# A 256-state scan: GpSimd relieved by VectorE every 64 steps, and LayerNorm's sums taken by ScalarE while it copies and squares

## The chip, the cores and the metric

The kernel runs on one core of a Trainium2 chip. A core has five engines that work side by side, each with its own queue of instructions in program order: PE (TensorE, matrix products), DVE (VectorE), ACT (ScalarE, functions of one operand), POOL (GpSimd) and SP (SyncE, which here only issues DMAs). Semaphores tie the queues together: an instruction waits at the head of its queue until what it needs is done, and everything behind it in that queue waits too. The metric is the device time of one execution in microseconds; lower is better. Before the change it is 21432.37 us (median of 3 runs, 21429.57 to 21440.76).

## The reference, cut to what matters

Two layers on an image batch of shape (4, 128, 64, 64), all in float32. Layer 0 is convolutions, a sort of patches and a scan with 16 states. Layer 1, in which the change lies, normalises tokens, runs a scan with 256 states for each of 256 channels over 4096 tokens, and then a long causal convolution with 16 filters:

```python
t = _to_tokens(x)                                  # (4, 4096, 128)
t = t + _L1_attn_ref(_ln_t(t), W_in, W_delta, W_B, W_C, W_out, A, D)
t = t + _L1_ffn_ref(_ln_t(t), ...)                 # the long convolution

def _ln_t(v, eps=1e-5):
    m = jnp.mean(v, axis=-1, keepdims=True)
    s = jnp.var(v, axis=-1, keepdims=True)
    return (v - m) / jnp.sqrt(s + eps)

# in _L1_attn_ref
deltaA = jnp.exp(jnp.einsum('bld,dn->bldn', delta, A))
deltaB = jnp.einsum('bld,bln->bldn', delta, Bv)
def step(state, inp):
    dA_i, dB_i, x_i, C_i = inp
    state = dA_i * state + dB_i * x_i[:, None, :]
    y = jnp.einsum('bdn,bn->bd', state, C_i)
    return (state, y)
```

## The kernel before, in words

`layer0_front` and `layer0_scan` come first and are not touched. `layer1` works on 32 parts: 4 batches by 8 chunks of 512 tokens, batches 0 and 1 one after the other, then batches 2 and 3 in turn chunk by chunk. A part has 256 steps, one for each channel d. A step scans one channel for all 256 states (128 partitions by 2 halves) over 512 tokens, so one instruction handles 1024 elements on each partition. The main loop (lines 1321 to 1370) issues, for step k:

- every second step, `fetch` (SP): the DMA that spreads two rows of delta over all partitions into `dlb` (4 buffers), for step k+8;
- at every half part, `carry` (POOL): it multiplies and adds in the state left by the chunk before;
- every second step, `spread` (line 1212, POOL): the scan's inputs v for steps k+4 and k+5, u times delta, 2 x 2 x 511 elements on each partition; v has 3 buffers of two steps each. ScalarE's small copy (line 1216) then puts the carried column in;
- `lift` (line 1232, ACT): two exponentials that make the factors da of step k+1, in one of two PSUM buffers;
- `due` (ACT): copies of finished convolutions (line 1181) that have come due;
- a piece of the step before's contraction: every 8 steps give four groups of PE products (line 1252) and two copies ye by ACT (line 1258), which are spread over steps 0 to 5 of the following eight;
- `scan` (line 1235, DVE): the scan of step k itself, which needs v and da;
- at most one piece of the work "beside": the output of the last part and the preparation (`project`) of the next. This work is written as generators. A piece marked "mm" is issued at step 6 of a group of eight, one marked "post" at step 7, and one marked "free" at any step. All "mm" pieces share a single PSUM buffer, `mm`;
- matmuls of the long convolution (line 1169, PE), as many as a credit allows.

**Relief.** GpSimd need not make all of v. At steps k with k % 128 == 118, `spread` is told to make only the first of its two steps, and `relief` makes the other: ScalarE copies the row of delta into the PSUM buffer `mm` (line 1222), and VectorE multiplies it with u (line 1224). While a relief is under way ("helping"), the "mm" piece of that group waits for the next one.

**Normalisation.** `normalise` (lines 828 to 850) is called twice a part: once by `project` for the next part's tokens, once by `output` for the tokens that go to the convolution. PE transposes the tokens into PSUM, ScalarE copies them to SBUF (lines 874 and 998), VectorE takes mean and variance of 4 rows of 128 (`bn_stats`, `bn_aggr`, lines 833 and 835), ScalarE adds eps and turns the mean's sign (838, 840), GpSimd raises to the power -1/2 and multiplies (843, 844), and after five more pieces ScalarE scales and shifts (line 848). Before the first step the first preparation runs with nothing beside it, and after the last step so does the last output.

Of the kernel before, what the change touches and what calls it, by code (L numbers as in the profile page):

```python
# [8 lines left out]
F32 = mybir.dt.float32  # L9
# [762 lines left out]
def layer1(ctx: ExitStack, tc, ident, half, weights, phi, pqd, mud, x, omd, permd, x2, x3, out):  # L772
# [52 lines left out]
    def middle():  # L825
        return pm.tile([128, TS], F32, tag="mm", name="mm")

    def normalise(t):

        st = sm.tile([128, NT, 6], F32, tag="st", name="st")  # L830
        mv = sm.tile([128, NT, 2], F32, tag="mv", name="mv")
        for i in range(NT):
            nc.vector.bn_stats(st[:, i, :], t[:, i, :])
        for i in range(NT):
            nc.vector.bn_aggr(mv[:, i, :], st[:, i, :])
        yield "free"
        ve = sm.tile([128, NT], F32, tag="ve", name="ve")
        nc.scalar.activation(ve, mv[:, :, 1], AF.Identity, bias=eps)
        ms = sm.tile([128, NT], F32, tag="ms", name="ms")
        nc.scalar.activation(ms, mv[:, :, 0], AF.Copy, scale=-1.0)  # L840
        yield "free"
        rs = sm.tile([128, NT], F32, tag="rs", name="rs")
        nc.gpsimd.tensor_tensor(rs, ve, half[:, :NT], ALU.pow)
        nc.gpsimd.tensor_tensor(ms, ms, rs, ALU.mult)
        for _ in range(5):
            yield "free"
        for i in range(NT):
            nc.scalar.activation(
                t[:, i, :], t[:, i, :], AF.Identity, bias=ms[:, i : i + 1], scale=rs[:, i : i + 1]
            )  # L850
# [11 lines left out]
    def project(b, ch, into):  # L862


        u, c, gate, delta, af, vf = into
        xq = small()
        nc.sync.dma_start(xq, x2[b][:, bass.ts(ch, TS)])
        yield "mm"
        tp = middle()
        for i in range(NT):  # L870
            nc.tensor.transpose(tp[:, bass.ts(i, 128)], xq[:, bass.ts(i, 128)], ident)
        yield "post"
        tr = small()
        nc.scalar.copy(tr, tp)
        yield "free"
        tr = tr.rearrange("p (i c) -> p i c", i=NT)
        yield from normalise(tr)
        yield "mm"
        ps = middle()
        for i in range(NT):  # L880
            nc.tensor.transpose(ps[:, bass.ts(i, 128)], tr[:, i, :], ident)
        yield "post"
        xn = small()
        nc.scalar.copy(xn, ps)
        z = wide()
        for j in range(2):
            yield "mm"
            ps = middle()
            nc.tensor.matmul(ps, win[:, bass.ds(256 + 128 * j, 128)], xn, start=True, stop=True)
            yield "post"  # L890
            nc.scalar.copy(z[:, j, :], ps)
        yield "free"
        nc.scalar.activation(z, z, AF.Silu)
        nc.sync.dma_start(gate, z)
        xs = wide()
        for j in range(2):
            yield "mm"
            ps = middle()
            nc.tensor.matmul(ps, win[:, bass.ts(j, 128)], xn, start=True, stop=True)
            yield "post"  # L900
            nc.scalar.copy(xs[:, j, :], ps)
        for j in range(2):
            yield "mm"
            ps = middle()
            for k in range(2):
                nc.tensor.matmul(ps, wbd[:, k, bass.ts(j, 128)], xs[:, k, :], start=k == 0, stop=k == 1)
            yield "post"
            nc.vector.tensor_tensor(u[:, j, :], ps, xs[:, j, :], ALU.mult)
        wcs = small().rearrange("p (k n) -> p k n", k=2)
        nc.sync.dma_start(wcs, wc)  # L910
        for j in range(2):
            yield "mm"
            ps = middle()
            for k in range(2):
                nc.tensor.matmul(ps, wcs[:, k, bass.ts(j, 128)], xs[:, k, :], start=k == 0, stop=k == 1)
            yield "post"
            nc.scalar.copy(c[:, j, :], ps)
            yield "mm"
            ps = middle()
            for k in range(2):  # L920
                nc.tensor.matmul(
                    ps, wbd[:, k, bass.ds(256 + 128 * j, 128)], xs[:, k, :], start=k == 0, stop=k == 1
                )
            yield "post"
            dl = small()
            nc.scalar.copy(dl, ps)
            nc.sync.dma_start(delta[bass.ts(j, 128), :], dl)

            yield "mm"
            ps = middle()  # L930
            nc.tensor.matmul(ps[:, 0:128], dl[:, 0:1].broadcast_to((128, 128)), ident, start=True, stop=True)
            yield "post"
            for h in range(2):
                nc.scalar.activation(vf[:, h, bass.ts(j, 128)], ps[:, 0:128], AF.Copy, scale=u[:, h, 0:1])
            for h in range(2):
                nc.vector.tensor_tensor(af[:, h, bass.ts(j, 128)], ps[:, 0:128], at[:, h, bass.ts(j, 128)], ALU.mult)
        yield "free"
        nc.scalar.activation(af, af, AF.Exp)
# [30 lines left out]
    def output(b, ch, yt, gate):  # L969


        cols = bass.ts(ch, TS)
        xr = small()
        nc.sync.dma_start(xr, x2[b][:, cols])
        yk = wide()
        nc.sync.dma_start(yk, gate)
        for k in range(2):
            yield "mm"
            ps = middle()
            for i in range(NT):  # L980
                nc.tensor.transpose(ps[:, bass.ts(i, 128)], yt[:, i, bass.ts(k, 128)], ident)
            yield "post"
            nc.vector.tensor_tensor(yk[:, k, :], ps, yk[:, k, :], ALU.mult)
        yield "mm"
        ps = middle()
        for k in range(2):
            nc.tensor.matmul(ps, wo[:, k, :], yk[:, k, :], start=k == 0, stop=k == 1)
        yield "post"
        nc.vector.tensor_tensor(xr, xr, ps, ALU.add)
        yield "mm"  # L990
        pair = xr.rearrange("p (a q) -> p q a", q=2)
        tp = middle()
        for r in range(2):
            for i in range(2):
                nc.tensor.transpose(tp[:, bass.ts(2 * r + i, 128)], pair[:, r, bass.ts(i, 128)], ident)
        yield "post"
        tk = small()
        nc.scalar.copy(tk, tp)
        yield "free"
        yield from normalise(tk.rearrange("p (i c) -> p i c", i=NT))  # L1000
        yield "mm"
        if ch % 2 == 0:
            tokens[b, ch // 2] = sp.tile([128, 2, 4, 128], F32, tag="tok", name="tok", bufs=6)
        tok = tokens[b, ch // 2]
        ps = middle()
        nc.tensor.matmul(ps, flip, tk, start=True, stop=True)
        yield "post"
        nc.scalar.copy(tok[:, :, bass.ts(ch % 2, 2), :], ps.rearrange("p (r i c) -> p r i c", r=2, i=2))
        yield "mm"
        up = middle()  # L1010
        for i in range(NT):
            nc.tensor.transpose(up[:, bass.ts(i, 128)], tk[:, bass.ts(i, 128)], ident)
        mu = small()[:, 0:384].rearrange("p (i c) -> p i c", i=3)
        nc.sync.dma_start(mu, mud[:, (0, 1, 2, 2, 3, 3, 3, 3)[ch]])
        yield "post"
        ut = sm.tile([128, 2 + TS], F32, tag="t2", name="ut", bufs=3)
        nc.scalar.copy(ut[:, 2:].rearrange("p (a q) -> p q a", q=2), up.rearrange("p (q a) -> p q a", q=2))
        if ch:
            nc.scalar.copy(ut[:, 0:2], halos[b % 2])
        else:  # L1020
            nc.scalar.activation(ut[:, 0:2], ident[:, 0:2], AF.Copy, scale=0.0)
        nc.scalar.copy(halos[b % 2], ut[:, TS:])
        yield "mm"
        ps = middle()
        for i in range(3):
            nc.tensor.matmul(ps, mu[:, i, :], ut[:, bass.ds(2 - i, TS)], start=i == 0, stop=i == 2)
        yield "post"
        nc.vector.tensor_tensor(xr, xr, ps, ALU.add)
        nc.sync.dma_start(x3[b][:, cols], xr)
        if (b, ch) == (NB - 1, NCH - 2):  # L1030
            add([(b, 3, [(3, range(2))], True, False)])
        elif (b, ch) == (NB - 1, NCH - 1):
            add([(b, 3, [(3, range(2, 4))], True, True)])
        elif ch % 2:
            block(b, ch // 2)
# [285 lines left out]
    for k in range(-10, steps):  # L1321
# [7 lines left out]
        j = k + 4  # L1329
        if 0 <= j < steps and j % VD == 0:  # L1330

            mine = k % 128 == 118 and kind != "post"
            vs[j // VD] = spread(j % 256, dls[j // VD], ready[j // 256], VD - mine)
            if mine:
                helping = relief(vs[j // VD], dls[j // VD], ready[j // 256])
# [127 lines left out]
```

## Time and profile before

| What | us |
|---|---|
| median of the runs | 21432.37 |
| the profiled execution | 21431.38 |
| its span, first to last instruction | 21429.6 |
| from the first scan (L1235) to the last | 2801.4 to 21249.6 |
| L1235's scans, busy | 18006.6 |
| L1212's products on POOL, busy | 18244.4 |

A line of the profile names a group of instructions by its line in the kernel, its engine and operation, what it writes and reads, and the shape on partitions by elements. Busy time is the time in which at least one of the group ran; "mean" is the average length of one, and because an engine starts an instruction while the last one finishes, it is longer than the distance from one start to the next. Idle time is that of the engine just before these instructions, with what ended it. The chain of waits is followed back from the last instruction: at each step to what released it, or to the one before it on its engine.

### The profile page before, as it was taken

The numbers are of one execution on the slowest core, as the hardware profiler recorded it, in microseconds if no ns is written. First come the engines' busy times: TensorE is split into PE (matmuls) and PEld (weight loads), VectorE is DVE, ScalarE is ACT, GpSimd is POOL, SyncE is SP. The second block draws the span as 40 slices with busy tenths as digits, with TensorE's granted clock in tenths as the row PEclk, the third lists the DMA queues.
The fourth block names the chain that finished last, engine by engine and source line by source line (L and its number), as shares of the span: only waits on it lengthen the run. The fifth ranks groups of instructions, "written<-read, shape, count | busy, mean of one in ns | idle before, by whom it ended". The sixth has DMA issues, their size and how long they took to land.

```text
span 21429.6 us, 294489 instructions
## 1 busy us (share of the span) xinstructions
PE 17672.7 (82%) x99308; PEld 7756.7 (36%) x99308; DVE 20566.6 (96%) x11871; ACT 16044.5 (75%) x29620; POOL 20134.2 (94%) x5685
## 2 busy tenths in 40 slices
PE   7788854565858888886868999599999999999997
PEld 4344421222323333342323344243434434334434
DVE  7788889999999999999999999999999999999996
ACT  3777767777777777777777777787887787788875
POOL 2677789999999999999999999999999999999996
PEclk8999966776979999998979999799999999999999
DMA  1455544555756777766657777577777777777776
GB/s 69 126 139 141 140 151 153 175 179 165 218 171 221 221 224 220 221 212 191 209 181 220 230 237 236 171 236 232 237 232 229 232 234 232 233 233 230 231 231 186
DMA packets 2498780, 4302.24 MB, mean 201 GB/s; under 512 B 803272, under 2 KB 1321712, under 8 KB 2494192
## 3 DMA queue, kind: packets, MB, share of 16 engines
q1 hardware_dynamic: 2497264, 4283.40, 65.4%
q8 instruction: 784, 12.85, 0.2%
q14 instruction: 732, 6.00, 0.1%
HBM read 3658.98 MB, written 623.38 MB: 200 GB/s over the span
## 4 chain that ended last, share of the span: by engine, by line
DVE 57%; PE 14%; POOL 9%; ACT 9%; issue 8%; DMA 3%; SPq 0%; DVEq 0%; POOLq 0%; ACTq 0%
DVE s L1235 50%; POOL v L1212 8%; PE conv L1169 6%; ACT da L1232 5%; DVE states L562 3%; PE yp L1252 3%; DVE p L566 2%; PE fin L1111 1%; ACT f L554 1%; PE y L578 1%; DMA strip<-in_phi 1%; DMA dlb<-delta 1%; PE mm L471 1%; PE conv L104 0%; DVE v L1224 0%
## 5 line engine op out<-in xcount | busy, mean ns | idle before, releaser
L1212 POOL TENSOR_TENSOR v<-u,dlb 128x2044 f32<-128x2044 f32 (+1 forms) x4096 | 18244.4, 4517 | 91.7 <-DMA dlb<-delta 66.0
L1235 DVE TENSOR_TENSOR_SCAN s<-da,v 128x1024 f32<-128x1024 f32 x8192 | 18006.6, 2264 | 188.3 <-ACT da L1232 130.3
L1232 ACT ACTIVATE da<-dlb,at 128x511 f32<-128x511 f32 x16384 | 11302.9, 690 | 1990.3 <-DVE s L1235 1488.8
L1169 PE MATMUL conv<-strip,tok 128*128 128x512 f32 (+3 forms) x20480 | 8653.3, 550 | 59.0 <-DMA strip<-in_phi 58.5
L1252 PE MATMUL yp<-s,c 128*32 128x256 f32 x65536 | 4957.0, 432 | 2616.2 <-DVE s L1235 1136.7
L1169 PEld LDWEIGHTS conv<-strip,tok 128*128 128x128 f32 x20480 | 3667.2, 192 | 4156.2 <-issue 3715.8
L1252 PEld LDWEIGHTS yp<-s,c 128*32 128x32 f32 x65536 | 1964.4, 120 | 6395.3 <-issue 2085.0
L1216 ACT COPY v<-vf 128x4 f32<-128x4 f32 x4096 | 814.2, 199 | 2112.6 <-DVE s L1235 2093.6
L1111 PE MATMUL fin<-conved,pq 128*128 128x512 f32 (+1 forms) x3968 | 1793.6, 545 | 11.1 <-ACT sum L1132 5.9
L540 POOL TENSOR_TENSOR v<-dx,bcb 128x1024 f32<-128x1024 f32 x512 | 1207.2, 2358 | 436.9 <-DVE states L562 430.5
L562 DVE TENSOR_TENSOR_SCAN states<-f,v 128x1024 f32<-128x1024 f32 x512 | 1175.8, 2297 | 172.6 <-ACT f L554 123.7
L554 ACT ACTIVATE f<-dt,an 128x255 f32<-128x255 f32 x2048 | 973.5, 476 | 418.0 <-DVE states L562 367.2
L1258 ACT COPY ye<-yp 128x512 f32<-128x512 f32 x2048 | 1186.1, 579 | 23.3 <-PE yp L1252 22.6
L1181 ACT COPY conved<-conv 128x512 f32<-128x512 f32 (+1 forms) x1728 | 986.9, 571 | 236.6 <-PE conv L1169 234.0
L578 PE MATMUL y<-p,ident 128*128 128x512 f32 x2048 | 1006.7, 620 | 148.2 <-DVE p L566 143.2
L1111 PEld LDWEIGHTS fin<-conved,pq 128*128 128x128 f32 x3968 | 664.2, 192 | 384.6 <-issue 284.2
L566 DVE TENSOR_TENSOR p<-states,bcb 128x1024 f32<-128x1024 f32 x512 | 626.9, 1224 | 41.1 <-DVE states L562 3.1
L578 PEld LDWEIGHTS y<-p,ident 128*128 128x128 f32 x2048 | 369.4, 195 | 680.9 <-issue 356.3
L471 PE MATMUL mm<-ow,yg 128*32 128x128 f32 x2048 | 283.1, 298 | 106.9 <-ACT om L475 105.4
L471 PEld LDWEIGHTS mm<-ow,yg 128*32 128x32 f32 x2048 | 236.6, 139 | 213.6 <-ACT om L475 128.5
L405 PE MATMUL mm<-xin,taps 128*128 128x512 f32 x512 | 236.6, 605 | 28.3 <-DVE f L384 14.4
L447 POOL TENSOR_TENSOR e<-e,e 128x1024 f32<-128x1024 f32 x32 | 75.1, 2346 | 191.0 <-ACT e L445 191.0
(242 smaller groups left out, 5948.1 us busy)
## 6 DMA issues: line engine op xcount, KB each, us to landing
dlb<-delta SPq DMA_DIRECT2D x4096, 512.0 KB, 4.2
strip<-in_phi SPq DMA_DIRECT2D x1536, 448.0 KB, 4.8
yd<-ye SPq DMA_DIRECT2D x2048, 256.0 KB, 4.1
strip<-in_phi SPq DMA_DIRECT2D x1088, 256.0 KB, 4.4
bcb<-bcd SPq DMA_DIRECT2D x1024, 256.0 KB, 4.1
pq<-pqd SPq DMA_DIRECT2D x1472, 64.0 KB, 3.8
yt<-yd SPq DMA_DIRECT2D x4096, 4.0 KB, 3.4
pq<-pqd SPq DMA_DIRECT2D x256, 128.0 KB, 3.9
```

Of the source, the lines that this page charges most:

```text
L540: nc.gpsimd.tensor_tensor(v, ready[n][2][:, :, bass.ts(i, SUB)].unsqueeze(1).broadcast_to((128, 2, 2, SUB)), bc[:, 0].unsqueeze(2).broadca ...
L554: nc.scalar.activation(factors[j % 2][:, a, k, 1:], ready[n][1][:, k, SUB * i + 1 : SUB * i + SUB], AF.Exp, scale=an[:, k, 2 * g + a : 2 * ...
L562: nc.vector.tensor_tensor_scan(states.rearrange(flat), factors[j % 2].rearrange(flat), v.rearrange(flat), 0.0, ALU.mult, ALU.add)
L566: nc.vector.tensor_tensor(p, states, bc[:, 1].unsqueeze(2).broadcast_to((128, 2, 2, SUB)), ALU.mult)
L578: nc.tensor.matmul(t.rearrange("p k t -> p (k t)"), ident, p[:, a].rearrange("p k t -> p (k t)"), start=g == 0 and a == 0, stop=False, ski ...
L1111: nc.tensor.matmul(fin[:, bass.ds(c0, w)], pq[:, n, :], u[:, bass.ds(c0, w)], start=begin and n == 0, stop=end and not partly, skip_group_ ...
L1169: nc.tensor.matmul(ps[:, skip:], tok[:, 1 - r if side else r, j, :], strip[:, bass.ds(c0 - lo, TS - skip)], start=which == 0 and j == js[0 ...
L1212: nc.gpsimd.tensor_tensor(v[:, 0:n, :, 1:], ready[0][:, :, 1:].unsqueeze(1).broadcast_to((128, n, 2, TS - 1)), dl[:, 0:n, 1:].unsqueeze(2) ...
L1232: nc.scalar.activation(da[:, h, 1:], dl[:, d % VD, 1:], AF.Exp, scale=at[:, h, d : d + 1])
L1235: nc.vector.tensor_tensor_scan(s[:, d % GD].rearrange("p h t -> p (h t)"), da.rearrange("p h t -> p (h t)"), v[:, d % VD].rearrange("p h t ...
L1252: nc.tensor.matmul(yp[i // 2][bass.ts(q, 32), i % 2], c[:, h, t], s[:, :, h, t], start=h == 0, stop=h == 1)
L1258: nc.scalar.copy(ye, yp[j].rearrange("p i d t -> p i t d"))
```

## The change

There are two edits. In the main loop a relief now comes every 64 steps (k % 64 == 54) and not every 128. In `normalise`, ScalarE's copy from PSUM is now made in four Identity activations, each of which also adds up its row; four Square activations, biased by the negative mean, one in each of four steps, add up the squares; the variance and eps follow from these sums in one small activation. VectorE's `bn_stats` and `bn_aggr` go, and so do the two copies of the callers, whose PSUM tile is now handed to `normalise`.

```diff
-    def normalise(t):
-
-        st = sm.tile([128, NT, 6], F32, tag="st", name="st")
-        mv = sm.tile([128, NT, 2], F32, tag="mv", name="mv")
+    def normalise(t, ps):
+
+        sums = sm.tile([128, 2, NT], F32, tag="st", name="st")
         for i in range(NT):
-            nc.vector.bn_stats(st[:, i, :], t[:, i, :])
+            nc.scalar.activation(t[:, i, :], ps[:, bass.ts(i, 128)], AF.Identity, accum_out=sums[:, 0, i : i + 1])
+        yield "free"
+        ms = sm.tile([128, NT], F32, tag="ms", name="ms")
+        nc.scalar.activation(ms, sums[:, 0, :], AF.Copy, scale=-1.0 / 128)
         for i in range(NT):
-            nc.vector.bn_aggr(mv[:, i, :], st[:, i, :])
+            yield "free"
+            sq = sm.tile([128, 128], F32, tag="sq", name="sq", bufs=1)
+            nc.scalar.activation(
+                sq, t[:, i, :], AF.Square, bias=ms[:, i : i + 1], accum_out=sums[:, 1, i : i + 1]
+            )
         yield "free"
         ve = sm.tile([128, NT], F32, tag="ve", name="ve")
-        nc.scalar.activation(ve, mv[:, :, 1], AF.Identity, bias=eps)
-        ms = sm.tile([128, NT], F32, tag="ms", name="ms")
-        nc.scalar.activation(ms, mv[:, :, 0], AF.Copy, scale=-1.0)
+        nc.scalar.activation(ve, sums[:, 1, :], AF.Identity, bias=eps, scale=1.0 / 128)
         yield "free"
...
         tr = small()
-        nc.scalar.copy(tr, tp)
-        yield "free"
         tr = tr.rearrange("p (i c) -> p i c", i=NT)
-        yield from normalise(tr)
+        yield from normalise(tr, tp)
...
         tk = small()
-        nc.scalar.copy(tk, tp)
-        yield "free"
-        yield from normalise(tk.rearrange("p (i c) -> p i c", i=NT))
+        yield from normalise(tk.rearrange("p (i c) -> p i c", i=NT), tp)
...
-            mine = k % 128 == 118 and kind != "post"
+            mine = k % 64 == 54 and kind != "post"
             vs[j // VD] = spread(j % 256, dls[j // VD], ready[j // 256], VD - mine)
```

## The prediction, made before the changed kernel ran

> **What bounds the kernel now.** Read in this order: the page's busy shares and chain, busy times by stage, groups, a stretch of the timeline. From the page:
>
> ```profile
> PE 17672.7 (82%) x99308; PEld 7756.7 (36%) x99308; DVE 20566.6 (96%) x11871; ACT 16044.5 (75%) x29620; POOL 20134.2 (94%) x5685
> ...
> DVE 57%; PE 14%; POOL 9%; ACT 9%; issue 8%; DMA 3%; SPq 0%; DVEq 0%; POOLq 0%; ACTq 0%
> DVE s L1235 50%; POOL v L1212 8%; PE conv L1169 6%; ACT da L1232 5%; DVE states L562 3%; PE yp L1252 3%; DVE p L566 2%; PE fin L1111 1%; ACT f L554 1%; PE y L578 1%; DMA strip<-in_phi 1%; DMA dlb<-delta 1%; PE mm L471 1%; PE conv L104 0%; DVE v L1224 0%
> ```
>
> DVE (VectorE) and POOL (GpSimd) look full, and the chain passes mostly through DVE's scan. The stages of the 256-state scan say more (microseconds of each engine, instructions in brackets):
>
> ```profile
> core 0: us, PE busy (x) PEld busy (x) DVE busy (x) ACT busy (x) POOL busy (x), PEclk, DMA share, GB/s
> 3000.00:12000.00 9000.00, 6642.12 (x42178) 2806.89 (x42182) 8927.65 (x4443) 6767.80 (x12456) 8978.62 (x2119) 0.85 0.64 198
> 14500.00:17000.00 2500.00, 2392.35 (x13415) 1031.04 (x13412) 2466.66 (x1235) 1995.19 (x3715) 2492.99 (x591) 0.99 0.75 233
> 19000.00:21200.00 2200.00, 2095.90 (x11923) 918.30 (x11923) 2165.56 (x1073) 1776.49 (x3279) 2184.30 (x515) 1.00 0.76 230
> ```
>
> POOL is busy 99.6 to 99.8% in every stage, DVE 98.4 to 99.2%, ACT (ScalarE) 75 to 81%, PE 74% and then 95 to 96%. The groups (busy us, mean ns | idle before, what ended it) of DVE, POOL and ACT:
>
> ```profile
> L1235 DVE TENSOR_TENSOR_SCAN s<-da,v 128x1024 f32<-128x1024 f32 x8192 | 18006.6, 2264 | 188.3 <-ACT da L1232 130.3 <-POOL v L1212 42.2
> ...
> L1224 DVE TENSOR_TENSOR v<-u,mm 128x1022 f32<-128x1022 f32 x64 | 76.2, 1190 | 0.0
> ...
> L833 DVE BATCH_NORM_STATS2 st<-t 128x6 f32<-128x128 f32 x256 | 54.0, 271 | 20.8 <-ACT t L874 19.4 <-ACT t L998 1.5
> ...
> L835 DVE BATCH_NORM_AGGREGATE mv<-st 128x2 f32<-128x6 f32 x256 | 23.0, 150 | 0.0
> ```
>
> ```profile
> L1212 POOL TENSOR_TENSOR v<-u,dlb 128x2044 f32<-128x2044 f32 (+1 forms) x4096 | 18244.4, 4517 | 91.7 <-DMA dlb<-delta 66.0 <-DVE s L1235 24.8
> ...
> L843 POOL TENSOR_TENSOR rs<-ve,half 128x4 f32<-128x4 f32 x64 | 66.4, 1037 | 73.1 <-ACT ms L840 38.5 <-ACT ve L838 34.6
> ...
> L1205 POOL TENSOR_TENSOR af<-af,last 128x256 f32<-128x256 f32 x56 | 42.8, 763 | 0.0
> L1206 POOL TENSOR_TENSOR vf<-vf,af 128x256 f32<-128x256 f32 x56 | 40.6, 725 | 4.4
> ```
>
> ```profile
> L1232 ACT ACTIVATE da<-dlb,at 128x511 f32<-128x511 f32 x16384 | 11302.9, 690 | 1990.3 <-DVE s L1235 1488.8 <-DMA yt<-yd 57.0 <-DMA strip<-in_phi 31.3
> ...
> L848 ACT ACTIVATE t<-t,ms,rs 128x128 f32<-128x128 f32 x256 | 104.7, 480 | 2.7 <-POOL ms L844 2.7
> ...
> L1222 ACT COPY mm<-dlb 128x512 f32<-128x512 f32 x64 | 36.9, 576 | 0.0
> ...
> L193 ACT ACTIVATION_READ_ACCUMULATOR f<-sum,b 128x1 f32 x32 | 5.8, 182 | 0.0
> ```
>
> Durations overlap their neighbours, so I take prices from start to start:
>
> ```profile
> 9998.36 39.34 DVE L1235 TENSOR_TENSOR_SCAN s<-da,v 128x1024 f32<-128x1024 f32 x18
> 10037.62 0.66 DVE L908 TENSOR_TENSOR u<-mm,t 128x512 f32<-128x512 f32 x1
> 10038.20 17.54 DVE L1235 TENSOR_TENSOR_SCAN s<-da,v 128x1024 f32<-128x1024 f32 x8
> ...
> 9998.86 62.86 POOL L1212 TENSOR_TENSOR v<-u,dlb 128x2044 f32<-128x2044 f32 x14
> ```
>
> 18 scans end to end take 39.26 us before the next operation starts (2.181 us each), 14 products v take 62.86 us (4.490 for two steps, 2.245 a step). So GpSimd is slower per step than the scan. DVE's extras fill the difference, or it waits for v.
>
> Sums for one part (256 steps; 32 parts, first scan at 2801.4 us, last at 21249.6 us: 18450 us, 576.6 a part):
> - POOL: 126 products x 4.49 + 2 halves x 2.31 (median) = 570.4; the powers and products of two normalisations 2 x (1.04 + 0.20) = 2.5; carries 2 x (0.76 + 0.73) = 3.0. Sum 575.9 of 576.6.
> - DVE: 256 x 2.181 = 558.4; the extras (L1224 2.4, L833 and L835 2.4, six evacuations together) 9.6 as start-to-start times. Sum 568.0. The other 8.6 are waits. Scan by scan, comparing each start with the later of its v and its da: 106 us in all for v, in 763 mostly tiny waits, 151 us for da in 182, and some 1 us a part of jitter. (The group row's 42.2 and 130.3 leave out the 0.08 us of overlap that a waiting scan loses.)
>
> By halves of the scan, in us a part: parts 0 to 15 take 575.8, with 4.3 for v and 2.8 for da; parts 16 to 31 take 577.2, with 2.4 for v and 6.7 for da, where the convolution's copies crowd ACT and PE is nearly full. In both halves POOL never rests while DVE waits for v: **POOL is the bound, and DVE is 2 to 4 us a part behind it.**
>
> **What the skill says.** GPSIMD Engine Reference, "3.1 Elementwise": a two-input fp32 tensor_tensor of 2048 elements takes 4497 ns; the trace agrees (4.49 us for 2044). Perfetto Trace Analysis, "GPSIMD Engine Instruction", wants such spans timed from start to start, as done here. SBUF — State Buffer, "SBUF: two separate sides": VectorE and GpSimd lock each other out only when VectorE uses a 2-port mode or two SBUF inputs. The added VectorE product reads u from SBUF and the copied row from PSUM, so it should not slow POOL; the trace agrees: beside L1224 a half product keeps its 2.32 us (median). ScalarE: Activation LUTs, "What ACT_TABLE_LOAD costs", is the price list used below: 186 ns + 0.833 ns an element, 93 ns more for each per-partition pointer operand, back-to-back overlap 93 ns. Trace: L848 (128 elements, two pointers) 480 ns against 479 by that rule.
>
> **The change, part by part.**
> (1) Relief every 64 steps: 64 more steps whose second half DVE makes. POOL loses 2 x (4.49 - 2.31) = 4.36 us a part, 139 us in all, from an engine without slack. DVE gains 2 x 1.11 (L1224 start to next start; mean 1.19) = 2.2 us a part. ACT gets 2 copies of 0.58 (L1222), at step 6 of a group of eight, where little else lies; each takes one of the slots in which PE's side products are issued.
> (2) bn_stats and bn_aggr leave DVE: 512 instructions. One normalisation takes 4 x 0.193 + 4 x 0.08 = 1.1 us from start to start, two a part: -2.2 us. This pays for (1) on DVE almost exactly, so DVE's own load is unchanged.
> (3) ACT's copy (0.58) becomes 4 Identity with sums, then 4 Square with sums. Identity reads PSUM, no pointer: 186 + 107 = 293 ns by the page (estimate), 0.20 start to start. Reading the accumulator adds 0.089: in the first layer the read starts 0.617 after L193's start, and the next operation 0.089 after the read. So 4 x 0.29 = 1.16. Square has one pointer: 0.29 + 0.09 = 0.38, 4 times, one a step. Bounds for an Identity: 0.25 (L934, from PSUM) to 0.385 (L848) before the read, so 0.29 to 0.47.
> When does ACT make DVE late? A lift (two L1232) takes 1.41 of a 2.18 us step, so 0.77 is left, and the two da buffers let a step run over by another 0.65 before the scan waits. On before: 4 L848 at 0.385 and a 0.11 copy leave the lift 0.82 late and cost a 0.17 stall, as the records show. The sums' step: 1.16 + 0.11 - 0.77 - 0.05 = 0.45, below 0.65: no stall, unless a convolution copy (0.5) falls in it, about one step in 8 in the first half and one in 3.3 in the second. The squares' steps hold at most a square, a ye copy and a small copy: 0.99, over by 0.2, paid back in the next step. I take 0.2 us a part of new stall in the first half, 0.5 in the second. At 0.47 an accumulating operation the sums' step stalls by 0.5, and it is 1.3 a part.
> (4) Moves. The normalisation's last step moves from step 7 to step 3 of the next group, before the same slot at step 6, so PE's next product is not later for it; the two more reliefs move what follows by one slot (8 steps), then two. In the changed kernel's own order the last piece of preparation is issued at step 215 instead of 199; the next part's rows are fetched from step 248. The DMAs are as many as before (4096 dlb, 64 delta and so on); the convolution's matmuls after the last scan also (128).  GpSimd's power waits for ve, issued one step before, as now. No table load is added (211 in both).
> (5) Where nothing covers: the preparation ahead of the first scan and the output after the last. There copy, bn and ve of 0.58 + 1.1 + 0.3 become 1.16 + 0.1 + 1.52 + 0.2, +1 us each, with hand-overs +4 in all at most; I take +3.
>
> **What is late next.** POOL falls to 571.5 (mean parts had up to 3.5 us of waits for a row's DMA: 66 us in all). DVE without waits for v, with new stalls: first half 575.8 - 4.3 + 0.2 = 571.7; second half 577.2 - 2.4 + 0.5 = 575.3. Both engines are level in the first half, and they alternate: carries fall at steps 118 and 246, the Silu's table loads (2.4 us stall) once a part, a relief every 64 steps moves 3.3 us of lead, and v's ring holds about 4.4. So I leave 1.2 us a part of waits for v in the first half, and 0.6 in the second, where POOL has room. Gain: 16 x (575.8 - 572.9) + 16 x (577.2 - 575.9) = 46 + 21 = 67, less 3: **64 us**. The profiled execution took 21431.4 (its span 21429.6), the median of the runs is 21432.4, 1 us apart, so the forecast is 21368.
>
> **The rivals.**
> - *Full gain:* all of POOL's 139 us is saved, if ACT's stalls shrink as the order shifts. Against: the second half's stalls for da (6.7 a part) are not POOL's. The 106 us and a few more: 21432 - 115 = 21317.
> - *DVE or ACT is the bound anyway:* waits for v vanish, but come back as waits for da, since a step no longer stretched by v leaves ACT less room; PE at 95% holds ye and the copies back. For it: 6.7 us a part. Then only half of the first half's gain stays: 21432 - 20 = 21412.
> - *Slower:* an accumulating activation cannot overlap with its read. The sums' step then has 4 x (0.39 + 0.18 + a drain of about 0.2), some 3 us on ACT's in-order queue, ahead of the lift for the next scan: stall 1.6, and each square 0.77, which fills its step's room and adds about 1 a normalisation in the first half and 2 in the second. Twice a part: 5 and 7 us against 3.1 and 1.8 gained: +30 and +83, 21545 at the full price. It decides from 106 / 32 = 3.3 us of new stall a part. Against it: L193's 0.089. A milder one ends near 21490.
> - *It does not do what it says:* excluded; the order shows 128 reliefs for 64, and no bn instruction in this scan.
>
> **Numbers.** About 0.2% (43 us) is what a measurement here can tell from no change. Forecast 0.60, of which a sixth lies within 43 us; full gain 0.10; bound anyway 0.15; slower 0.15, most of it beyond 43 us. Faster 0.60, same 0.25, slower 0.15. The likeliest one's own range is 21325 to 21410; the range with 8 in 10 takes in most of the full gain and of the bound case: 21310 to 21430.
>
> **What would show it.** Right: L1212 with 128 halves and about 139 us less busy time; L1235's wait for POOL v well under 42 us; POOL's busy share down to about 99%, with waits for DVE's scan; L1235's wait for ACT da 130 to 150; the reads at about 0.09 from start to start. Wrong: waits for da near 250, an Identity with sums that lasts over 0.5 us, or POOL still at 99.7% with a v slower than 4.49.

## The result, and the profile after

| What | before | after |
|---|---|---|
| median of 20 runs of each, us | 21436.17 | 21405.07 |
| the profiled execution's span, us | 21429.6 | 21403.1 |
| a part, parts 0 to 15, us | 575.79 | 573.88 |
| a part, parts 16 to 31, us | 577.23 | 577.20 |

The ratio is 0.9986, with a 95% interval of 0.998 to 0.9992: 31 us faster. The forecast was 64 us faster, so the direction was right and the time lies in the range, but half of the gain did not come. By parts the whole gain is in the first half (16 x 1.91 = 31 us, where 46 were forecast), and the second half gave nothing (21 were forecast). (The two profiled executions are 26.5 us apart: 31 in the parts, less some 4 that the two ends cost.)

First the page of the kernel after: the busy shares, then the chain by engine and by line.

```profile
PE 17645.8 (82%) x99308; PEld 7753.1 (36%) x99308; DVE 20524.2 (96%) x11423; ACT 16192.4 (76%) x30644; POOL 19986.7 (93%) x5685
...
DVE 60%; PE 14%; ACT 10%; issue 8%; POOL 4%; DMA 3%; SPq 0%; DVEq 0%; POOLq 0%; ACTq 0%
DVE s L1235 53%; PE conv L1169 6%; ACT da L1232 5%; DVE states L562 3%; POOL v L1212 3%; PE yp L1252 3%; DVE p L566 2%; PE fin L1111 1%; ACT f L554 1%; DVE v L1224 1%; DMA strip<-in_phi 1%; PE y L578 1%; ACT ye L1258 1%; PE mm L471 1%; DMA dlb<-delta 0%
```

POOL does 147 us less, and the chain passes through its products for 3% of the span in place of 8%. DVE takes the chain over. POOL is no longer the bound, as the stages show as well (busy time of each engine in each stretch, instructions in brackets):

```profile
core 0: us, PE busy (x) PEld busy (x) DVE busy (x) ACT busy (x) POOL busy (x), PEclk, DMA share, GB/s
3000.00:12000.00 9000.00, 6624.72 (x42295) 2809.56 (x42288) 8926.64 (x4248) 6864.31 (x12995) 8938.77 (x2127) 0.85 0.64 199
14500.00:17000.00 2500.00, 2386.97 (x13442) 1028.64 (x13444) 2468.96 (x1173) 2015.07 (x3856) 2477.68 (x592) 1.00 0.76 233
19000.00:21200.00 2200.00, 2096.40 (x11930) 917.51 (x11933) 2162.98 (x1025) 1793.93 (x3392) 2166.70 (x515) 0.99 0.76 230
```

POOL's share is 99.3, 99.1 and 98.5%. So it has slack now, and yet the scan still waits for it. The groups of DVE (busy us, mean ns | idle before, and what ended it), then of POOL:

```profile
L1235 DVE TENSOR_TENSOR_SCAN s<-da,v 128x1024 f32<-128x1024 f32 x8192 | 17972.6, 2292 | 194.4 <-ACT da L1232 143.3 <-POOL v L1212 42.0
...
L1224 DVE TENSOR_TENSOR v<-u,mm 128x1022 f32<-128x1022 f32 x128 | 155.2, 1212 | 0.0
```

```profile
L1212 POOL TENSOR_TENSOR v<-u,dlb 128x2044 f32<-128x2044 f32 (+1 forms) x4096 | 18097.2, 4473 | 208.9 <-DMA dlb<-delta 131.9 <-DVE s L1235 65.0 <-POOL v L1212 6.4
```

The wait for v stands at 42.0 us where it was 42.2. This row counts idle time only, and hides what changed. Scan by scan, before lost 35 us in 33 waits for v of half a microsecond or more, and 71 us in some 750 tiny ones; after loses 35 us in 24 long ones, and 22 us in some 240 tiny ones. The change took away tiny waits, which fits a POOL that could just not keep up. The long ones stayed.

On POOL, the waits for the scan (a free v buffer) rose from 24.8 to 65.0 us, which is what an engine with slack shows; but the waits for a row of delta rose too, from 66.0 to 131.9. In both sums one wait lies ahead of the first scan, that for the first row of all (timeline of POOL, before, then after; in brackets the idle time before and its releaser):

```profile
2796.85 13.41 POOL L1212 TENSOR_TENSOR v<-u,dlb 128x2044 f32<-128x2044 f32 x3 [43.81 <-DMA dlb<-delta]
2805.20 4.50 POOL L1212 TENSOR_TENSOR v<-u,dlb 128x2044 f32<-128x2044 f32 x1 [45.72 <-DMA dlb<-delta]
```

Without it the waits for rows rose from 22 to 86 us, fourfold. This is where the missing gain has to be looked for.

ScalarE's sums were as cheap as forecast. A stretch of its timeline ahead of the first scan (start us, length us; first line with its idle time before):

```profile
2754.23 0.28 ACT L832 ACTIVATE t<-mm 128x128 f32<-128x128 f32 x1 [8.34 <-PE mm L875]
2754.41 0.20 ACT L832 ACTIVATION_READ_ACCUMULATOR t<-mm 128x1 f32 x1
2754.50 0.27 ACT L832 ACTIVATE t<-mm 128x128 f32<-128x128 f32 x1
```

The read starts 0.18 us after its Identity, and the next Identity 0.09 after the read: 0.27 for this pair, with no drain in between. Over all 192 such pairs the median is 0.25.

**Where the time went.** As in the prediction, each scan's start was compared with the later of its v and its da. In us a part, worked out from the records (the scans themselves take 558.4 in every row; what is left over is jitter):

| us a part, first half / second half | period | waits for da | waits for v | DVE's other work |
|---|---|---|---|---|
| before | 575.79 / 577.23 | 3.88 / 7.39 | 4.25 / 2.36 | 8.99 / 8.87 |
| after | 573.88 / 577.20 | 3.90 / 8.11 | 2.15 / 1.46 | 9.26 / 9.14 |
| forecast for after | 572.9 / 575.9 | +0.2 / +0.5 | 1.2 / 0.6 | no change |

(Waits for da are counted more widely here than in the prediction, which had 2.8 and 6.7 for before and left the tiny waits to jitter. With only waits above 0.06 us before has 2.8 and 6.6, and after 3.3 and 7.4.) Waits for v are 0.95 and 0.86 us a part above the forecast, together 29 us of the 36 by which the parts miss their forecast (16 x 0.98 + 16 x 1.30). DVE's other work adds 0.27 a part, 9 us; ScalarE's new stalls are, in this table's count, 3 us below the forecast in the first half and 4 above it in the second.

**One late row.** The waits for v in the first half are not spread out: of 34.4 us, 33.1 lie in steps 64 to 127 of a part, and most of it in parts 2, 4, 6, 12 and 14, with 4 to 5.4 us each, while parts 1, 3, 7, 8, 10 and 15 have at most 0.6. In these parts POOL stands still once, at step 88. In part 4 (timeline of POOL, then of DVE):

```profile
5284.21 9.00 POOL L1212 TENSOR_TENSOR v<-u,dlb 128x2044 f32<-128x2044 f32 x2
5298.73 9.01 POOL L1212 TENSOR_TENSOR v<-u,dlb 128x2044 f32<-128x2044 f32 x2 [5.52 <-DMA dlb<-delta]
```

```profile
5273.73 8.82 DVE L1235 TENSOR_TENSOR_SCAN s<-da,v 128x1024 f32<-128x1024 f32 x4
5282.47 0.69 DVE L1028 TENSOR_TENSOR t<-t,mm 128x512 f32<-128x512 f32 x1
5283.07 17.55 DVE L1235 TENSOR_TENSOR_SCAN s<-da,v 128x1024 f32<-128x1024 f32 x8
5303.29 4.47 DVE L1235 TENSOR_TENSOR_SCAN s<-da,v 128x1024 f32<-128x1024 f32 x2 [2.67 <-POOL v L1212]
```

POOL waits 5.52 us for a row; DVE lives on the v buffers that were already filled until 5300.6 and then waits 2.67. Why was the row late? SP's timeline over the same time (issues of DMAs; the length is that of issuing):

```profile
5278.00 0.32 SPq L1259 DMA_DIRECT2D yd<-ye  x1
5279.87 0.32 SPq L1196 DMA_DIRECT2D dlb<-delta  x1
5283.19 0.32 SPq L1029 DMA_DIRECT2D x<-t  x1
5283.61 0.37 SPq L871 DMA_DIRECT2D t<-x  x1
5284.03 4.31 SPq L1275 DMA_DIRECT2D yt<-yd  x8
5288.39 0.43 SPq L1077 DMA_DIRECT2D pq<-pqd  x1
5288.86 0.91 SPq L1083 DMA_DIRECT2D strip<-in_phi  x2
5289.81 0.43 SPq L1077 DMA_DIRECT2D pq<-pqd  x1
5290.29 0.43 SPq L1083 DMA_DIRECT2D strip<-in_phi  x1
5290.83 1.31 SPq L1196 DMA_DIRECT2D dlb<-delta  x2
```

From 5280.2 to 5283.2 SP stands at line 1029, the write of x3: it needs VectorE's sum of line 1028, which DVE reaches only after its scans, and which ends at 5283.16. Behind that write the program queues the load of line 871, eight reads of y, filters and strips, and only then the row for steps 88 and 89. The row is issued at 5290.83, right behind these transfers, and lands late as well (chain of waits: start, length, what):

```profile
5290.83 7.75 DMA dlb<-delta
5298.57 0.02 issue
5298.60 0.04 POOLq L1212
5298.64 0.09 issue
5298.73 4.53 POOL v L1212
5303.27 0.02 issue
5303.29 4.48 DVE s L1235 x2
```

7.75 us against a median of 4.2 for these rows. Such gaps on POOL, of 4 to 7 us, are found in eight parts (2, 4, 6, 12, 14, 16, 19 and 23), 45.6 us in all. The kernel before had the same event one group earlier, at step 80, with 1.0 to 3.5 us in ten parts, 24 us in all. So the change did not make it. It moved it by 8 steps, and a POOL that runs further ahead comes to the late row sooner and waits longer for it: the rows just ahead of the late one had lain ready for 8.1 us (median) when POOL took them in before, and for 5.1 in after, and the pauses grew by 1.6 to 4.5 us (the eight parts without part 16).

**Why in these parts.** SP stands at the write for 2.5 to 4.1 us in most parts, and in eight of those (1, 3, 7, 8, 10, 11, 15 and 18) POOL pauses for at most 0.3 us. What sets the eight apart is what follows the write. Worked out from the records of after (medians, us; part 0 has no such write, and for five rows the landing is not on record):

| loads of filters and strips between the write and the row | parts | SP stands at the write | from the write to the row's issue | row in flight | POOL's pause, least to most |
|---|---|---|---|---|---|
| none | 12 | 2.3 | 4.8 | 4.4 | 0 to 0.6 |
| one or two | 11 | 3.0 | 5.7 | 6.1 | 0 to 3.2 |
| four to six | 8 | 3.5 | 7.3 | 7.4 | 4.1 to 6.3 |

The last row of this table is exactly the eight parts. In `output`, the call that gives the convolution new work stands right behind the write, in every second chunk; in parts 4, 6, 12, 14 and 19 the convolution's matmuls (line 1169) had stood still for 310 to 780 us when it came. Its first loads then go out in one burst, ahead of the row. Where it was still at work, as in parts 8 and 10, there is no burst. So three things add up: a write that waits for VectorE, the reads and loads that are issued behind it, and a longer flight.

### The profile page after: what moved, and what is told of

It reads as the page before. It is cut to its first block, busy times and chain, and to the rows that moved or that the text cites. A ratio compares the mean times of both kernels' runs of the same rounds, so it can differ in the third digit from the quotient of the medians.

```text
span 21403.1 us, 295158 instructions
## 1 busy us (share of the span) xinstructions
PE 17645.8 (82%) x99308; PEld 7753.1 (36%) x99308; DVE 20524.2 (96%) x11423; ACT 16192.4 (76%) x30644; POOL 19986.7 (93%) x5685
## 3 DMA queue, kind: packets, MB, share of 16 engines
q14 instruction: 736, 6.03, 0.1%
## 4 chain that ended last, share of the span: by engine, by line
DVE 60%; PE 14%; ACT 10%; issue 8%; POOL 4%; DMA 3%; SPq 0%; DVEq 0%; POOLq 0%; ACTq 0%
DVE s L1235 53%; PE conv L1169 6%; ACT da L1232 5%; DVE states L562 3%; POOL v L1212 3%; PE yp L1252 3%; DVE p L566 2%; PE fin L1111 1%; ACT f L554 1%; DVE v L1224 1%; DMA strip<-in_phi 1%; PE y L578 1%; ACT ye L1258 1%; PE mm L471 1%; DMA dlb<-delta 0%
## 5 line engine op out<-in xcount | busy, mean ns | idle before, releaser
L1212 POOL TENSOR_TENSOR v<-u,dlb 128x2044 f32<-128x2044 f32 (+1 forms) x4096 | 18097.2, 4473 | 208.9 <-DMA dlb<-delta 131.9
L1235 DVE TENSOR_TENSOR_SCAN s<-da,v 128x1024 f32<-128x1024 f32 x8192 | 17972.6, 2292 | 194.4 <-ACT da L1232 143.3
```

Of the source, the lines that this page charges most:

```text
L1212: nc.gpsimd.tensor_tensor(v[:, 0:n, :, 1:], ready[0][:, :, 1:].unsqueeze(1).broadcast_to((128, n, 2, TS - 1)), dl[:, 0:n, 1:].unsqueeze(2) ...
L1235: nc.vector.tensor_tensor_scan(s[:, d % GD].rearrange("p h t -> p (h t)"), da.rearrange("p h t -> p (h t)"), v[:, d % VD].rearrange("p h t ...
```

## The experiments

My theory when these began: the missing gain is the late row; the write of x3 in front of it is the cause. The rivals: the two halves of the change do not fit together (one of them alone gives all of the 31 us, or costs), DVE or ScalarE is the bound in any case, or too little was moved from POOL. Each run was timed together with the kernel before on the same chip; its medians were 21443.67 in the group of e1 to e4, 21442.15 for e5, e6 and e8, and 21442.61 for e9 and e10, each group on another chip. "Against before" below is the difference from the median of the same group.

| Kernel | median us | ratio to before (95%) | against before | v waits | da waits | DVE's other work |
|---|---|---|---|---|---|---|
| e1_relief_only | 21443.22 | 0.9999 (0.9991 to 1.0007) | -0.5 | 1.05 | 5.62 | 11.15 |
| e2_sums_only | 21433.82 | 0.9995 (0.9987 to 1.0003) | -9.9 | 4.92 | 5.76 | 6.99 |
| e3_after_late_write | 21360.67 | 0.9961 (0.9948 to 0.9975) | -83.0 | 0.46 | 6.03 | 9.21 |
| e4_before_late_write | 21424.27 | 0.9991 (0.9982 to 0.9999) | -19.4 | 2.87 | 5.85 | 8.93 |
| e5_relief_48 | 21393.88 | 0.9978 (0.997 to 0.9986) | -48.3 | 0.15 | 5.65 | 10.67 |
| e6_split_scale | 21355.44 | 0.9959 (0.9945 to 0.9972) | -86.7 | 0.44 | 5.46 | 9.21 |
| e8_tanh_gate | 21305.41 | 0.9937 (0.9925 to 0.995) | -136.7 | 0.48 | 2.60 | 10.33 |
| e9_sums_late | 21412.63 | 0.9986 (0.9979 to 0.9992) | -30.0 | 4.18 | 5.83 | 6.99 |
| e10_relief_late | 21399.79 | 0.998 (0.9972 to 0.9988) | -42.8 | 0.13 | 5.46 | 11.15 |

The last three columns are us a part over all 32 parts, worked out as above; before has 3.31, 5.64 and 8.93, after has 1.81, 6.01 and 9.20.

### The two halves of the change, each alone

e1 is the kernel before with the relief every 64 steps; e2 is the kernel after with the relief every 128:

```diff
# e1, on before
-            mine = k % 128 == 118 and kind != "post"
+            mine = k % 64 == 54 and kind != "post"
# e2, on after
-            mine = k % 64 == 54 and kind != "post"
+            mine = k % 128 == 118 and kind != "post"
```

> The relief every 64 steps alone, with the old normalisation (bn_stats on VectorE). Theory (GpSimd and VectorE are level, so each half of the change needs the other): GpSimd loses 4.4 us a part, but VectorE gains 2.2 us a part and becomes the bound; no gain, -10 to +25 us against before (21436). L1212's busy time falls by about 147 us, as with both. Rival (the relief brings the whole gain): about -31 us.

> ScalarE's sums alone, with the old relief every 128 steps. Theory (GpSimd stays the bound, VectorE's 2.0 us a part that go turn into waits for v): -10 to +10 us against before; L1235's waits for v grow from 3.3 us to about 5 us a part. Rival (VectorE is the bound, so 64 us less of bn on it count, less 12 us of new ScalarE stall): about -50 us.

Neither gives a gain that can be told from none. (L1212's busy time fell by 131 us in e1, where 147 were expected.) The groups of e1, DVE's and POOL's:

```profile
L1235 DVE TENSOR_TENSOR_SCAN s<-da,v 128x1024 f32<-128x1024 f32 x8192 | 17951.7, 2263 | 175.6 <-ACT da L1232 140.1 <-POOL v L1212 27.0 <-issue 0.3
```

```profile
L1212 POOL TENSOR_TENSOR v<-u,dlb 128x2044 f32<-128x2044 f32 (+1 forms) x4096 | 18113.1, 4477 | 225.1 <-DMA dlb<-delta 126.1 <-DVE s L1235 84.1 <-POOL v L1212 8.2
```

With the relief alone the scan waits less for v (2.26 us a part less), but DVE spends just that on its new products (2.22 more). With the sums alone DVE gets 1.94 us a part of room, and waits for POOL instead (1.61 more). Each half moves the time to the other engine; together they save it. Note that the waits for rows, 126.1 us (43.7 of them for the first row of all), are in e1 already: they come with the relief, not with the sums.

### The write of x3 two steps later

The edit lets two more steps pass between VectorE's sum and the write, so that the fetch of the row goes to SP first. All that follows the write in the program comes later with it: the load of line 871 and the call that gives the convolution new work. The eight reads of y stay ahead of the row. e3 makes it on the kernel after, e4 on the kernel before:

```diff
         nc.vector.tensor_tensor(xr, xr, ps, ALU.add)
+        yield "free"
+        yield "free"
         nc.sync.dma_start(x3[b][:, cols], xr)
```

> The changed kernel, with the DMA of x3 issued two steps later, so that SP issues the row for steps 88 and 89 before it waits for VectorE's sum (step 79). Theory A (the waits for v that remain come from this late row, in 9 parts of 32): waits for v fall from 58 us to about 25, the 4 to 6 us pauses of GpSimd at step 88 go, and the time falls to about 21375 (-30 against the changed kernel). Rival B (they come from GpSimd and VectorE taking turns in being ahead, with a ring of only three buffers): no change, within 8 us of the changed kernel.

> The kernel before, with the same later DMA of x3. Theory A: GpSimd is the bound there, so its 2 to 3.5 us pauses at step 80 (24 us in ten parts) are all on the path: about -22 us against before. Rival B: within 8 us of before.

SP's timeline of e3 in the same part, then POOL's (the edit shifts lines by 2: the fetch is line 1198, the write 1031):

```profile
5276.19 0.32 SPq L1198 DMA_DIRECT2D dlb<-delta  x1
5276.56 3.75 SPq L1277 DMA_DIRECT2D yt<-yd  x8
5280.52 0.34 SPq L1198 DMA_DIRECT2D dlb<-delta  x1
5280.96 1.27 SPq L1031 DMA_DIRECT2D x<-t  x1
5282.33 0.38 SPq L871 DMA_DIRECT2D t<-x  x1
5282.76 0.50 SPq L1079 DMA_DIRECT2D pq<-pqd  x1
5283.31 1.01 SPq L1085 DMA_DIRECT2D strip<-in_phi  x2
5284.37 0.43 SPq L1079 DMA_DIRECT2D pq<-pqd  x1
5284.85 0.43 SPq L1085 DMA_DIRECT2D strip<-in_phi  x1
5285.63 0.33 SPq L1198 DMA_DIRECT2D dlb<-delta  x1
```

```profile
5280.69 17.91 POOL L1214 TENSOR_TENSOR v<-u,dlb 128x2044 f32<-128x2044 f32 x4
```

The row for steps 88 and 89 is now issued at 5280.52, ahead of the write, lands at 5284.60, and POOL runs through with no pause. SP no longer stands at the write, and the convolution's burst of loads now lies ahead of the next row, for steps 90 and 91, without harm: in the eight parts POOL pauses at most 0.4 us for that row. So the burst alone does not make a row late. Whether it takes SP's 3 us at the write, or the burst and the eight reads of y ahead of the same row, these runs do not tell, because the edit changes both. The groups of e3, DVE's and POOL's:

```profile
L1237 DVE TENSOR_TENSOR_SCAN s<-da,v 128x1024 f32<-128x1024 f32 x8192 | 17945.8, 2263 | 171.3 <-ACT da L1234 145.7 <-POOL v L1214 16.6 <-issue 0.6
```

```profile
L1214 POOL TENSOR_TENSOR v<-u,dlb 128x2044 f32<-128x2044 f32 (+1 forms) x4096 | 18102.1, 4475 | 166.0 <-DVE s L1237 75.2 <-DMA dlb<-delta 68.9 <-POOL v L1214 11.0
```

Waits for rows fall from 131.9 to 68.9 us (without the first row of all, from 86 to 23), waits for v from 42.0 to 16.6, while POOL's busy time is as in the kernel after. On the kernel before the same edit is worth 19 us (interval 2 to 39), on the kernel after some 52 (83.0 less 31.1; their intervals, 54 to 112 and 17 to 43, do not overlap), more than the 30 expected. By these medians the late row cost some 33 us more after the change than before it. From e4 to e3, that is for the change itself with this row out of the way, it is 64 us.

### The two halves again, with the later write

e9 is e3 with the relief every 128 steps, e10 is e4 with the relief every 64: the same one-line edits as in e2 and e1.

> ScalarE's sums and the later DMA of x3, with the old relief every 128 steps. Theory (with the old relief GpSimd stays the bound, row late or not): as the sums alone (-10) and the later DMA on the kernel before (-19) together, about -30 us against before; waits for v stay above 4 us a part. Rival (with the row on time VectorE's saving counts by itself): -60 us or more.

> The relief every 64 steps and the later DMA of x3, with the old normalisation. Theory (VectorE is the bound, with 2 us a part more than in the changed kernel with the later DMA): waits for v fall from 1.05 to about 0.3 us a part, -20 to -30 us against before. Rival (the relief alone pays once the row is on time): -60 us or more.

The step from e4 is -11 us for the sums alone, -23 for the relief alone, -64 for both (from the column against before). (These are differences between groups of runs, and each of e4, e9 and e10 has an interval of 14 to 18 us to either side, e3 one of 29: the sums' -11 cannot be told from none.) The relief alone gained more than I had expected, 43 us against before and not 20 to 30; its waits for v are at 0.13 us a part, so nothing is left to win on POOL, and its DVE is full with 11.15 us of other work. The sums alone leave 4.18 of waits for v. Together they are worth nearly twice their sum, which fits two engines that stand level: what relieves one alone is soon stopped by the other.

### More relief

e5 is e3 with the relief every 48 steps:

```diff
-            mine = k % 64 == 54 and kind != "post"
+            mine = k % 48 == 38 and kind != "post"
```

> The changed kernel with the later DMA of x3 and a relief every 48 steps (5.3 a part in place of 4). Theory (after both, VectorE with its waits for da is the bound and waits for v are 0.5 us a part): each more relief costs VectorE 1.11 us, 1.33 x 1.11 x 32 = 47 us, less at most 15 us of waits for v that go: +30 to +47 us against the kernel with the later DMA alone (21361). Rival (GpSimd still bounds it): another 93 us of GpSimd's work go, so the time falls.

It is 35 us slower than e3, in the range expected. POOL's group:

```profile
L1214 POOL TENSOR_TENSOR v<-u,dlb 128x2044 f32<-128x2044 f32 (+1 forms) x4096 | 18015.6, 4445 | 279.8 <-DVE s L1237 169.9 <-DMA dlb<-delta 74.1 <-POOL v L1214 21.6
```

POOL does 87 us less than in e3, and waits 95 us more for the scan: DVE pays for work that POOL had time for. With the row on time DVE is the bound, and of the three distances run (128, 64 and 48 steps) 64 is the best. This rules out that too little was moved.

### What is late next: ScalarE

In e3 the scan's largest wait is for da. e6 puts the last normalisation's four activations in two steps instead of one, and e8 also removes the change of ScalarE's tables once a part: the Silu of the gate is computed as z (1 + tanh(z/2)), with W_out halved once at the start of the layer.

```diff
# e6, on e3, in the loop of the four scale activations of normalise
+            if i == 2:
+                yield "free"
# e8, on e6, in project
-            nc.scalar.copy(z[:, j, :], ps)
-        yield "free"
-        nc.scalar.activation(z, z, AF.Silu)
+            nc.scalar.activation(z[:, j, :], ps, AF.Tanh, scale=0.5)
+            nc.vector.scalar_tensor_tensor(z[:, j, :], z[:, j, :], 1.0, ps, ALU.add, ALU.mult)
# e8, at the start of layer1
+    nc.vector.tensor_scalar(wo, wo, 0.5, None, ALU.mult)
```

> The changed kernel with the later DMA of x3, and LayerNorm's four scaling activations spread over two steps. Theory (ScalarE's in-order queue stalls the scan where a step has more than 0.77 us beside the lift, plus 0.65): the stalls at steps 53 and 101, 0.17 us alone and 0.45 to 0.69 with a convolution copy, go: about -0.5 us a part, -10 to -20 us against the kernel with the later DMA alone. Rival (the stalls move on to the next step and GpSimd or PE takes their place): 0.

> As the split kernel, and the gate's Silu is made as z (1 + tanh(z/2)) with 1/2 put into the output weights: ScalarE's Tanh takes the place of a copy, needs no table load, and VectorE multiplies by z out of PSUM. Theory (VectorE and its waits for da are the bound): the 2.4 to 3 us stall at step 130 of each part goes, VectorE has 2 x 0.58 = 1.2 us a part more: -1.3 us a part, about -40 us against the split kernel. Rival (GpSimd bounds it by then): at most -15 us.

e6 is 4 us below e3, less than expected and within both intervals: its waits for da fell by 0.57 us a part, but that a gain came of it was not shown. e8 is 50 us below e6; the two intervals overlap a little, but no run of e8 was above 21316 us and none of e6 below 21339. Its DVE group:

```profile
L1239 DVE TENSOR_TENSOR_SCAN s<-da,v 128x1024 f32<-128x1024 f32 x8192 | 17941.0, 2261 | 71.3 <-ACT da L1236 51.6 <-POOL v L1216 14.5
```

The wait for da goes from 138.2 in e6 to 51.6 us. The profile of e8 has 147 table loads of 1.283 us where the others have 211: two fewer a part. DVE's two products cost 1.1 us a part, and still the sum is positive. e8 is the fastest kernel of this study, 0.9937 of before.

Not tried: a fourth buffer for v, moving the eight reads of y behind the row, and moving the convolution's first loads alone.

## Why the prediction was right or wrong

**Right: the bound and the relief (1).** POOL was the bound; 128 halves came, and 147 us of busy time went (139 forecast). POOL's share fell to about 99%, and its waits for the scan rose. One reading was off: POOL's share in the last stage of before is 99.3% (2184.30 of 2200), not 99.6% or more, so late in the second half POOL had some rest already.

**Right: ScalarE (3).** Identity with its read was 0.25 us (median) where 0.29 was taken, and the read of a square starts 0.30 us after it where 0.29 was taken; a read costs the 0.09. New stalls were 0.02 and 0.72 us a part against 0.2 and 0.5; counted as the prediction counted (waits above 0.06 us) they are 0.5 and 0.9, with less jitter in exchange. The slower rival needed a read that cannot overlap, and fell with these lines; so did "ScalarE is the bound anyway" for the whole, since the waits for v did not vanish and the wait for da (143.3 us) stayed inside the 130 to 150 forecast. In the second half, though, something like it came true: waits for v fell by 0.90 us a part, waits for da rose by 0.72 and DVE's work by 0.27, and nothing was gained. That the measured 21405 lies closer to this rival's 21412 than to the forecast's 21368 shows that the total alone would not have told them apart. The full gain, 115 us, fell as well: even with the row on time it is 83 with the edit counted in, since ScalarE's stalls did not shrink. The ends (5) were small as forecast: the first scan starts 8.3 us later, of which 4.6 lie in layer 0, which is the same in both, and what follows the last scan is 4 us shorter.

**Nearly right: what VectorE saves (2).** The bn instructions were worth 2.0 us a part, not 2.2, against 2.2 for the products: DVE's own work rose by 0.27 us a part, 9 us in all, where "almost exactly" had been zero.

**Wrong: the waits for v that stay, 1.2 and 0.6 us a part.** Measured were 2.15 and 1.46: 29 us, most of what was missing. The term was sized by an argument (carries, table loads, reliefs and the ring of v make the two engines alternate) and by no row of the profile. The runs put something else in its place: a single row of delta that comes late in some of the parts, because SP's queue holds it behind a write that waits for VectorE and behind the reads and loads that follow this write. With that row on time (e3) the waits are 0.37 and 0.55, below what I had taken for alternation, and the change is worth 64 us, the size of the forecast. That the same size comes out is partly chance: the forecast counted from before with its late row, the 64 from e4 without it; and in e3 the first half is faster than forecast (572.27 against 572.9) and the second slower (576.44 against 575.9).

**Wrong: the moves (4).** They were judged on PE, ScalarE and POOL only. The DMAs were counted, and their number was right, but SP's order around step 79 was not followed. The profile of before had the clue, POOL's waits for a row, which "what is late next" entered as slack that would stay as it is. It also read them wrongly: of the 66 us, 44 are one wait ahead of the first scan, and 22 lie in the scan. These 22 became 86.

**The signs.** "L1235's wait for POOL v well under 42" was the sign that failed (42.0), and it pointed straight to the failing term: the row holds mostly the long waits, and these had not changed.

Still open: how the late row's delay divides between SP's standing at the write, the reads of y and the convolution's loads, and how much of the 7.75 us in flight is due to the transfers issued just before. That the range held is in part luck: 21405 lies 5 us inside its upper end of 21410 in the likeliest case, with half of the gain missing.

## What to carry to other kernels

When an engine is relieved, list what its waits were already, DMA waits above all, and read them as what will stop it when it runs ahead, not as slack. Look at each such wait one by one, not at its sum: two thirds of the 66 us here were a single wait at the start. Follow the in-order DMA queue past the change too: a write that waits for a result holds up every load behind it. Here such a wait of about 3 us cost POOL at most 0.6 where only the reads of y followed it, and 4 to 6 us where a burst of other loads came behind them; issuing both two steps later gave 19 us on the kernel before and some 52 on the kernel after, more than the change itself. Where two engines stand level, work moved between them pays only together with work taken away.

## What the runs showed of the hardware that was not expected

- The records of VectorE are longer in the profile of after than in all others: a scan's mean is 2292 ns, against 2260 to 2266 in the others, and L1224's is 1212 against 1188 to 1191 in before, e1, e3 and e5, while scans still start 2.18 us apart. Durations of two profiles are not to be subtracted; starts are.
- A row of 512 KB that takes 4.2 us at the median took 7.75 when issued right behind fifteen other DMAs. At step 88 of after the medians are 4.4 us behind ten, 6.1 behind eleven or twelve, and 7.4 behind fourteen to sixteen.
- Two squares with sums that write the same buffer stand 0.53 us apart ahead of the first scan, though a square's read starts 0.31 after it and an Identity's read gives way to the next after 0.09. In the loop there is one square a step.
